# Row sums and turned attention outputs by way of device memory, in a fused graph-attention kernel

## The chip, the cores and the metric

One of the eight cores of a Trainium2 chip runs the whole program. The metric is the device time of one execution in microseconds (us). A core has five engines with instruction streams of their own: TensorE (PE, with PEld for its weight loads), VectorE (DVE), ScalarE (ACT), GpSimd (POOL) and SyncE (SP), whose queue issues nearly all transfers here. All times below are in us where no unit is named.

## The reference

Two layers on x of shape (32, 512, 512), with one 512 x 512 adjacency matrix for all 32 sequences. The first is masked attention with eight heads of 64, the second a graph convolution; each is followed by a residual and a layer norm.

```python
q, k, v = x @ Wq + bq, x @ Wk + bk, x @ Wv + bv          # eight heads of 64
scores = einsum('bihd,bjhd->bhij', q, k) / sqrt(64) + where(adj == 0, -1e9, 0)
weights = softmax(scores, axis=-1)
x = layernorm(x + einsum('bhij,bjhd->bihd', weights, v))
y = einsum('nm,bmd->bnd', adj, x)
x = layernorm(x + einsum('bnd,do->bno', y, W1) + b1)
```

## The kernel before

The kernel works through the 32 sequences b. The eight heads are taken in pairs hp (two heads of 64 lanes fill 128 partitions) and two pairs make a group g, so there are 64 groups (b, g), numbered i in the main loop. Every engine's order is the order in which the Python code emits instructions; there is no scheduler behind it. In one pass of the loop over groups:

- `attend(b, hp)`: 16 matmuls (32 instructions, L585 for the two pairs) multiply the exponentials e with the values into one PSUM bank, which holds the output transposed (head lanes on partitions, queries along the row). There are eight banks, used in a ring.
- `fold_squares(b, hp)`: the sum over the keys of the exponentials es (already added over the four key blocks on GpSimd, L576) still lies across partitions. VectorE transposes es in 32 x 32 squares (L618) and adds up each run of 32 (L620), which leaves, for every query, four parts on four different partitions, 32 apart.
- `turn_out(b, hp)`: VectorE transposes the output in 32 x 32 squares into `attT` (L601); 16 transfers on SP (L606), each of one square column of 16 KB, carry the squares to their partitions in `rows`. That is 32 transfers in a group.
- `scores` for the next group: 32 matmul instructions (L561) into 16 banks, which VectorE masks and evacuates (L563) and ACT exponentiates (L565).
- `add_up(b, g)`: four small matmuls (eight instructions, L628) with a constant 0/1 matrix `fold` (four identity matrices of 32 stacked) add the four parts into a PSUM bank. VectorE takes the reciprocal (L631) and adds the sums into `sums` (L632); GpSimd adds the reciprocals into `inverses` (L633). `sums` and `inverses` are looked at once, at the end (`judge`, L662 to L669), to decide whether a slower general kernel has to run.
- then the slot of the group, a list of units: projections of sequence b + 1 (L353), convolutions and aggregations of sequence b - 1 (L353, L472), statistics (L415), splits into high and low parts (L441, L445), `scale_rows` (ACT multiplies `rows` by the inverses, L644) and `add_rows` (GpSimd adds them to x, L648).

Two places differ from this. In the first group the second fold comes after the scores, and `add_up` is put at place 8 of the slot. In the last sequence both folds of its second group lie in the slots, and after the last slot come `add_up(31, 1)`, `last_residual` (L654 to L657, multiplying by the inverse), the statistics of the first norm, and the last aggregation and convolution. `load_squares` (L248) reads the x of two sequences ahead in 32-wide columns, `store` and `load` (L456, L233) write a finished sequence and read x for the residual; all three are on SP.

Of the kernel before, what the change touches and what calls it, by code (L numbers as in the profile page):

```python
# [37 lines left out]
FP = mybir.dt.float32  # L38
# [4 lines left out]
ALU = mybir.AluOpType  # L43
AX = mybir.AxisListType
# [3 lines left out]
P = 128  # L48
# [10 lines left out]
SQ = 32  # L59
XIN = 4  # L60
GROUP = 4
# [146 lines left out]
def fast_kernel(ctx: ExitStack, tc, verdict, x, adj, Wq, bq, Wk, bk, Wv, bv, W1, b1, out):  # L208
    nc = tc.nc
    B, N, D = x.shape  # L210
    H = Wq.shape[1] // HD
    HP = H // 2
    NB = N // P
# [4 lines left out]
    consts = ctx.enter_context(tc.tile_pool(name="consts", bufs=1))  # L218
    work = ctx.enter_context(tc.tile_pool(name="work", bufs=2))
    psum = ctx.enter_context(tc.tile_pool(name="psum", bufs=1, space=bass.MemoryType.PSUM))  # L220
    ctx.enter_context(tc.manual_schedule())

    def bank(*shape):

        return psum.tile([P, *shape], FP, name="bank", tag="bank", bufs=8)
# [34 lines left out]
    ident = consts.tile([P, P], FP, name="ident")  # L260
    make_identity(nc, ident)
    ones = consts.tile([P, 1], FP, name="ones")
    nc.gpsimd.memset(ones, 1.0)

    fold = consts.tile([P, SQ], FP, name="fold")
    nc.gpsimd.tensor_add(fold, ident[:, 0:SQ], ident[:, SQ:2 * SQ])
    for i in (2, 3):
        nc.gpsimd.tensor_add(fold, fold, ident[:, i * SQ:(i + 1) * SQ])
    eps = consts.tile([P, 1], FP, name="eps")
    nc.gpsimd.memset(eps, EPS)  # L270
    zero = consts.tile([P, 1], FP, name="zero")
# [2 lines left out]
    sums = consts.tile([P, NB, GROUP], FP, name="sums")  # L274
# [115 lines left out]
    def flips(b):  # L390

        return [(turn_squares if b else x_transpose, b, c) for c in range(NB)] + [(sum_rows, b)] if b < B else []

    def projections(b):


        if b >= B:
            return []
        units = [(project, b, which, i) for which in "qkv" for i in ORDER]
        for n in (5, 12):  # L400
            units[n:n + 4] = units[n + 2:n + 4] + units[n:n + 2]
        return units
# [136 lines left out]
    def aggregation(b):  # L539


        return [[(f, b, d) for d in range(DB)] if b >= 0 else [] for f in (split, aggregate)]

    def convolution(b):
        return [(convolve, b, i) for i in (1, 2, 5, 6, 7, 3, 4)] if b >= 0 else []


    E, ES, OUT, AT, ROWS, SQUARES, PART, INVERSE = {}, {}, {}, {}, {}, {}, {}, {}
    PAIRS = GROUP // 2

    def scores(b, g):
# [41 lines left out]
    def turn_out(b, hp):  # L593

        po = OUT.pop((b, hp))
        at = AT[b, hp] = work.tile([P, N], FP, name="attT")
        if (b, hp // PAIRS) == (B - 1, HP // PAIRS - 1):
            nc.scalar.activation(at, po, AF.Copy)
            return

        nc.vector.transpose(at, po)  # L601
        turned = at.rearrange("p (c j f) -> p c j f", c=NB, j=P // SQ)
        rows = ROWS[b, hp] = work.tile([P, NB, P], FP, name="rows")
        for i in range(P // SQ):
            for j in range(P // SQ):
                nc.sync.dma_start(rows[j * SQ:(j + 1) * SQ, :, i * SQ:(i + 1) * SQ],  # L606
                                  turned[i * SQ:(i + 1) * SQ, :, j, :])

    def fold_squares(b, hp):

        if hp % PAIRS == 0:
            PART[b, hp // PAIRS] = work.tile([P, GROUP, N // SQ], FP, name="part", bufs=1)
        if (b, hp // PAIRS) == (B - 1, HP // PAIRS - 1):

            square = work.tile([P, 2, N], FP, name="v", bufs=3)
        else:
            square = SQUARES.pop((b, hp))
        nc.vector.transpose(square.rearrange("p s n -> p (s n)"), ES.pop((b, hp)).rearrange("p s n -> p (s n)"))  # L618
        heads = slice(2 * (hp % PAIRS), 2 * (hp % PAIRS) + 2)
        nc.vector.tensor_reduce(PART[b, hp // PAIRS][:, heads, :], square.rearrange("p s (j f) -> p s j f", f=SQ),  # L620
                                axis=AX.X, op=ALU.add)

    def add_up(b, g):

        part = PART.pop((b, g)).rearrange("p h (j i) -> p i j h", i=P // SQ)
        pm = bank(NB, GROUP)
        for i in range(P // SQ):
            nc.tensor.matmul(pm[i * SQ:(i + 1) * SQ, :, :], fold, part[:, i, :, :], start=True, stop=True,  # L628
                             tile_position=(0, i * SQ))
        inverse = INVERSE[b, g] = work.tile([P, NB, GROUP], FP, name="inverse")  # L630
        nc.vector.reciprocal(inverse, pm)  # L631
        nc.vector.tensor_add(sums, pm, sums)  # L632
        nc.gpsimd.tensor_add(inverses, inverses, inverse)  # L633

    def inverse_of(b, hp):
# [37 lines left out]
    def run(units):  # L673
        for unit in units:
            unit[0](*unit[1:])
# [4 lines left out]
    pm = bank(P)  # L680
    for _ in range(7):
        nc.tensor.matmul(pm, still, still, start=True, stop=True)
    turned, first = flips(0), projections(0)
# [38 lines left out]
    def norm(t, which):  # L722

        if t - which < 0:
            return []
        lo, hi = which * NB, (which + 1) * NB
        return [(square_root, t, slice(lo, hi)), (invert_root, t, slice(lo, hi))] + [
            (normalise, t, slot) for slot in range(lo, hi)]

    def folds(b, g):  # L730
        return [(fold_squares, b, hp) for hp in range(g * PAIRS, (g + 1) * PAIRS)]
# [9 lines left out]
    def merge(units, behind):  # L741

        merged = []
        for k in range(max(len(units), len(behind))):
            merged += units[k:k + 1] + (behind[k] if k < len(behind) else [])
        return merged

    def units_of(b):

        made, turned = projections(b + 1), flips(b + 2)  # L750
        splits, gathered = aggregation(b - 1)
        old, seen = norm(b - 1, 1), survey(b - 2)

        fresh, young = ([(statistics, b - 1, 0, c) for c in range(NB)], norm(b - 1, 0)) if b else ([], [])
        scaled, added = residuals(b, 0)
        if b == B - 1:


            first, second = folds(b, 1)
            behind = [fresh[:2], fresh[2:], young[:1] + scaled[:1], young[1:3], young[3:5] + [first],  # L760
                      young[5:] + splits[:1], splits[1:] + scaled[1:]]
            return [merge(convolution(b - 2), behind), [second] + added + gathered]

        ready = [(turn_over, b)] if b > 1 else []
        if old:
            behind = [seen[:2], seen[2:], old[:2], old[2:4] + fresh[:2], old[4:] + ready + fresh[2:]] + [
                [u] for u in young]
        elif b:
            behind = [ready + fresh] + [[u] for u in young]
            behind += [[(look_for_low_half, c)] for c in range(NB)]  # L770
        else:
            behind = [[]] + [[(sum_weights, w1, n)] for n in range(4)]
        behind += [[] for _ in range(11 - len(behind))]
        behind += [splits[:1], scaled + added, splits[1:2]]
        slot0 = merge(made[:16], behind)
        values = made[16:]
        scaled, added = residuals(b, 1)
        slot1 = values[:3] + gathered[:1] + splits[2:3] + gathered[1:2] + splits[3:] + scaled[:1]
        slot1 += values[3:]
        if b == B - 2 > 0:  # L780
            slot1 += [(load, B - 1)]
        slot1 += gathered[2:3] + turned[:1] + gathered[3:]
        convolved = convolution(b - 1) if b < B - 2 else []
        slot1 += merge(convolved, [scaled[1:] + added[:1] + turned[1:2], turned[2:3], turned[3:4], [], [], [],
                                   added[1:] + turned[4:]])
        return [slot0, slot1]

    GROUPS = H // GROUP
    groups = [(b, g) for b in range(B) for g in range(GROUPS)]
    for i, (b, g) in enumerate(groups):  # L790
        for hp in range(g * PAIRS, (g + 1) * PAIRS):
            attend(b, hp)
            if i < len(groups) - 1 and (i or hp == 0):
                fold_squares(b, hp)
            turn_out(b, hp)
            if i == hp == 0:
                run(flips(1))
        if g == 0:
            slots = units_of(b)
        if i < len(groups) - 1:  # L800
            later = scores(*groups[i + 1])
            if i:
                add_up(b, g)
            else:
                fold_squares(b, 1)
                slots[0].insert(8, (add_up, b, g))
        if g == 0 and b + 2 < B:
            load_squares(b + 2)
        for unit in slots[g]:
            run([unit])  # L810
            if unit[0] == convolve or unit[0] == project and unit[3] == 7:
                run(later)
                later = []
        run(later)
        later = []
# [41 lines left out]
    for unit in last:  # L857
# [13 lines left out]
        if unit[2] == 7:  # L871
            pm = bank(N)
# [41 lines left out]
```

## Time and profile before

| | us |
|---|---|
| median of three runs | 2749.52 (2749.11 to 2749.98) |
| the profiled execution's own time | 2749.17 |
| its span in the trace | 2747.3 |
| TensorE busy | 2729.7 (99%), granted clock 0.998 |
| VectorE, GpSimd, ScalarE busy | 2064.8, 1903.0, 1411.4 |
| transfers: share of the 16 DMA engines | 23.0%, mean 52 GB/s |

The span is what the trace covers; the execution's own time has 1.9 more around it. A busy time of TensorE is not a measure of full use, because matmuls overlap and their ends are modelled: the start of the next one says more. In a timeline a line reads: start, length of the group of instructions, engine, line of the program, operation, output<-inputs, shapes, number, and in brackets how long the engine stood idle before it and what ended that. In the list of transfers, the row transfers are 2016 of 16 KB with 1.8 from issue to landing, the column loads of x 496 of 64 KB with 2.4, and the four stores of 256 KB at the end 2.7.

### The profile page before, as it was taken

The numbers are of one execution on the slowest core, as the hardware profiler recorded it, in microseconds if no ns is written. First come the engines' busy times: TensorE is split into PE (matmuls) and PEld (weight loads), VectorE is DVE, ScalarE is ACT, GpSimd is POOL, SyncE is SP. The second block draws the span as 40 slices with busy tenths as digits, with TensorE's granted clock in tenths as the row PEclk, the third lists the DMA queues.
The fourth block names the chain that finished last, engine by engine and source line by source line (L and its number), as shares of the span: only waits on it lengthen the run. The fifth ranks groups of instructions, "written<-read, shape, count | busy, mean of one in ns | idle before, by whom it ended". The sixth has DMA issues, their size and how long they took to land.

```text
span 2747.3 us, 39383 instructions
## 1 busy us (share of the span) xinstructions
PE 2729.7 (99%) x12856; PEld 1911.3 (70%) x12856; DVE 2064.8 (75%) x3348; ACT 1411.4 (51%) x2459; POOL 1903.0 (69%) x1224
## 2 busy tenths in 40 slices
PE   9999999999999999999999999999999999999997
PEld 6676676766767767667676676676766767767666
DVE  6777777777777787777877777777777777777777
ACT  3455464554544655446555455454554644555454
POOL 4776677666867667777677676777666867667775
PEclk9999999999999999999999999999999999999999
DMA  5212211222212222122221222211222212222121
GB/s 149 32 28 62 56 29 45 57 62 57 44 30 56 61 59 54 19 57 60 60 57 23 51 59 61 56 27 47 58 62 57 43 30 56 62 58 49 25 59 50
DMA packets 592915, 142.20 MB, mean 52 GB/s; under 512 B 554560, under 2 KB 558656, under 8 KB 592704
## 3 DMA queue, kind: packets, MB, share of 16 engines
q1 hardware_dynamic: 592704, 139.63, 23.0%
q8 instruction: 103, 1.69, 0.3%
q14 instruction: 108, 0.88, 0.1%
HBM read 72.88 MB, written 33.55 MB: 39 GB/s over the span
## 4 chain that ended last, share of the span: by engine, by line
PE 98%; DVE 1%; DMA 0%; ACT 0%; issue 0%; SPq 0%; POOL 0%; DVEq 0%; ACTq 0%
PE bank L353 56%; PE bank L561 17%; PE bank L585 16%; PE bank L472 8%; PE bank L628 0%; DMA wq<-in_L_gnn_Wq_dram 0%; DVE bnst L415 0%; DVE xs L534 0%; DVE part L847 0%; PE bank L287 0%; POOL xs L532 0%; SPq L239 0%; ACT xT L430 0%; DVE stat L416 0%; DVE xT L534 0%
## 5 line engine op out<-in xcount | busy, mean ns | idle before, releaser
L565 ACT ACTIVATE e<-e 128x1024 f32<-128x1024 f32 x512 | 524.9, 1053 | 572.8 <-DVE e L563 537.5
L563 DVE SCALAR_TENSOR_TENSOR e<-gap,bank 128x512 f32<-128x512 uint8 x1024 | 617.7, 679 | 20.2 <-PE bank L561 20.2
L576 POOL TENSOR_TENSOR es<-es,e 128x1024 f32<-128x1024 f32 x256 | 618.3, 2415 | 20.1
L576 POOL TENSOR_TENSOR es<-e 128x1024 f32<-128x1024 f32 x128 | 316.2, 2470 | 328.2 <-ACT e L565 328.2
L561 PE MATMUL bank<-q,k 64*128 64x512 f32 x2048 | 463.0, 598 | 0.0
L585 PE MATMUL bank<-e,v 128*64 128x512 f32 x2048 | 453.6, 595 | 0.0
L353 PE MATMUL bank<-wv,xT 128*128 128x256 f32 x1792 | 405.4, 381 | 0.0
L353 PE MATMUL bank<-xT,wk 128*128 128x256 f32 x1792 | 402.9, 379 | 0.0
L353 PE MATMUL bank<-xT,wq 128*128 128x256 f32 x1792 | 400.8, 381 | 1.9 <-DMA wq<-in_L_gnn_Wq_dram 1.7
L353 PE MATMUL bank<-w,yT 128*128 128x256 f32 x1792 | 394.3, 380 | 3.5 <-DVE yT L509 3.5
L561 PEld LDWEIGHTS bank<-q,k 64*128 64x128 f32 x2048 | 203.4, 186 | 258.0 <-issue 152.2
L353 PEld LDWEIGHTS bank<-w,yT 128*128 128x128 f32 x1792 | 341.2, 191 | 52.0 <-DVE yT L509 3.9
L353 PEld LDWEIGHTS bank<-xT,wk 128*128 128x128 f32 x1792 | 340.2, 190 | 46.1
L353 PEld LDWEIGHTS bank<-xT,wq 128*128 128x128 f32 x1792 | 337.8, 190 | 48.9 <-issue 1.9
L353 PEld LDWEIGHTS bank<-wv,xT 128*128 128x128 f32 x1792 | 337.6, 190 | 47.6 <-DVE e L563 0.8
L644 ACT ACTIVATE rows<-rows,zero,inverse 128x64 f32<-128x64 f32 x1008 | 343.4, 427 | 4.6 <-DMA rows<-attT 4.6
L585 PEld LDWEIGHTS bank<-e,v 128*64 128x64 f32 x2048 | 141.4, 137 | 277.1 <-issue 275.7
L648 POOL TENSOR_TENSOR xs<-xs,rows 128x512 f32<-128x512 f32 x124 | 158.0, 1285 | 164.3 <-DMA xs<-in_x_dram 164.3
L565 ACT ACT_TABLE_LOAD x30 | 38.5, 1283 | 416.6 <-DVE e L563 416.6
L445 DVE TENSOR_TENSOR low<-xs,high 128x512 fp32r<-128x512 f32 x122 | 141.8, 1162 | 106.1 <-ACT high L441 106.1
L534 DVE TENSOR_TENSOR xs<-bank,xs 128x512 f32<-128x512 f32 x186 | 124.3, 682 | 96.8 <-PE bank L353 46.2
L430 ACT ACTIVATE xs<-xs,shift,rstd 128x512 f32<-128x512 f32 x248 | 181.9, 803 | 27.2 <-DVE shift L425 27.2
(128 smaller groups left out, 2963.3 us busy)
## 6 DMA issues: line engine op xcount, KB each, us to landing
rows<-attT SPq DMA_DIRECT2D x2016, 16.0 KB, 1.8
xin<-in_x_dram SPq DMA_DIRECT2D x496, 64.0 KB, 2.4
xs<-in_x_dram SPq DMA_DIRECT2D x31, 1024.0 KB, 5.1
out_dram<-xs SPq DMA_DIRECT2D x31, 1024.0 KB, 4.4
xin<-in_x_dram SPq DMA_DIRECT2D x4, 256.0 KB, 3.3
wq<-in_L_gnn_Wq_dram SPq DMA_DIRECT2D x2, 512.0 KB, 6.7
wk<-in_L_gnn_Wk_dram SPq DMA_DIRECT2D x2, 512.0 KB, 5.7
yT<-in_adj_dram SPq DMA_DIRECT2D x1, 1024.0 KB, 7.2
```

Source lines behind the costliest of these rows:

```text
L353: nc.tensor.matmul(pm[:, r, :], left[:, d, r * P:(r + 1) * P], right[:, d, :], start=(d == 0), stop=(d == 1))
L430: nc.scalar.activation(row, row, AF.Identity, bias=SHIFT[t][:, slot:slot + 1], scale=RSTD[t][:, slot:slot + 1])
L445: nc.vector.tensor_sub(LOW[b, d], cols, HIGH[b, d].bitcast(FP))
L472: nc.tensor.matmul(pm.rearrange("p a n -> p (a n)"), part, adjT[:, n % NB, :], start=(n == 0), stop=(n == 2 * NB - 1))
L534: nc.vector.tensor_add(block, pm, block)
L561: nc.tensor.matmul(ps[s], keys[:, j * P:(j + 1) * P], queries, start=True, stop=True)
L563: nc.vector.scalar_tensor_tensor(e[:, s, :], gap[:, j, :], NEG * root, ps[s], op0=ALU.mult, op1=ALU.add)
L565: nc.scalar.activation(e, e, AF.Exp, scale=1.0 / root)
L576: nc.gpsimd.tensor_add(ES[b, hp], ES[b, hp] if j > 1 else E[b, hp, 0], E[b, hp, j])
L585: nc.tensor.matmul(po[s * HD:(s + 1) * HD, :], values, e[:, s, :], start=(j == 0), stop=(j == NB - 1))
L644: nc.scalar.activation(part, part, AF.Identity, bias=zero, scale=inverse[:, c, s:s + 1])
L648: nc.gpsimd.tensor_add(cols, cols, ROWS.pop((b, hp)))
```

## The change

A pool `passing` of tiles in device memory is added. The turned output `attT` is stored there whole (one transfer), and a new `fetch_rows` reads it back in four transfers, one for each 32 partitions, each of 512 pieces of 128 bytes. The four parts of the row sums take the same way: a store after the second fold, and a new `fetch_parts` with four reads, after which each partition holds all four parts of its queries. `add_up` is then a reduction on VectorE; the matrix `fold` and its matmuls are gone, and so is their PSUM bank. `sums` is added from the reduced tile in SBUF instead of from PSUM. For the new layout of the parts each reduction of 1024 elements becomes two of 512. In the main loop the fetches are emitted around the second `turn_out`, and `add_up` moves from directly behind the scores to place 3 of the slot (place 8 stays in the first group). In the last group the fetch follows the last fold, and `add_up` keeps its place.

```diff
-    fold = consts.tile([P, SQ], FP, name="fold")
-    nc.gpsimd.tensor_add(fold, ident[:, 0:SQ], ident[:, SQ:2 * SQ])
-    for i in (2, 3):
-        nc.gpsimd.tensor_add(fold, fold, ident[:, i * SQ:(i + 1) * SQ])
...
         nc.vector.transpose(at, po)
-        turned = at.rearrange("p (c j f) -> p c j f", c=NB, j=P // SQ)
+        TURNED[b, hp] = passing.tile([P, N], FP, name="turned")
+        nc.sync.dma_start(TURNED[b, hp], at)
+
+    def fetch_rows(b, hp):
         rows = ROWS[b, hp] = work.tile([P, NB, P], FP, name="rows")
-        for i in range(P // SQ):
-            for j in range(P // SQ):
-                nc.sync.dma_start(rows[j * SQ:(j + 1) * SQ, :, i * SQ:(i + 1) * SQ],
-                                  turned[i * SQ:(i + 1) * SQ, :, j, :])
+        turned = TURNED.pop((b, hp)).rearrange("(i r) (c j f) -> j r c i f", r=SQ, c=NB, f=SQ)
+        for j in range(P // SQ):
+            nc.sync.dma_start(rows[j * SQ:(j + 1) * SQ, :, :].rearrange("p c (i f) -> p c i f", f=SQ), turned[j])
...
-        heads = slice(2 * (hp % PAIRS), 2 * (hp % PAIRS) + 2)
-        nc.vector.tensor_reduce(PART[b, hp // PAIRS][:, heads, :], square.rearrange("p s (j f) -> p s j f", f=SQ),
-                                axis=AX.X, op=ALU.add)
+        for s in range(2):
+            nc.vector.tensor_reduce(part[:, :, :, 2 * (hp % PAIRS) + s].rearrange("p i c -> p c i"),
+                                    square[:, s, :].rearrange("p (c i f) -> p c i f", c=NB, f=SQ), axis=AX.X,
+                                    op=ALU.add)
+        if hp % PAIRS == PAIRS - 1:
+            PASSED[b, hp // PAIRS] = passing.tile([P, P // SQ, NB * GROUP], FP, name="passed")
+            nc.sync.dma_start(PASSED[b, hp // PAIRS], part.rearrange("p i c h -> p i (c h)"))
+
+    def fetch_parts(b, g):
+
+        part = PART[b, g].rearrange("p a c h -> p a (c h)")
+        passed = PASSED.pop((b, g)).rearrange("(a r) i x -> i r a x", r=SQ)
+        for i in range(P // SQ):
+            nc.sync.dma_start(part[i * SQ:(i + 1) * SQ, :, :], passed[i])

     def add_up(b, g):

-        part = PART.pop((b, g)).rearrange("p h (j i) -> p i j h", i=P // SQ)
-        pm = bank(NB, GROUP)
-        for i in range(P // SQ):
-            nc.tensor.matmul(pm[i * SQ:(i + 1) * SQ, :, :], fold, part[:, i, :, :], start=True, stop=True,
-                             tile_position=(0, i * SQ))
         inverse = INVERSE[b, g] = work.tile([P, NB, GROUP], FP, name="inverse")
-        nc.vector.reciprocal(inverse, pm)
-        nc.vector.tensor_add(sums, pm, sums)
+        nc.vector.tensor_reduce(inverse, PART.pop((b, g)).rearrange("p a c h -> p c h a"), axis=AX.X, op=ALU.add)
+        nc.vector.tensor_add(sums, sums, inverse)
+        nc.vector.reciprocal(inverse, inverse)
         nc.gpsimd.tensor_add(inverses, inverses, inverse)
...
             first, second = folds(b, 1)
+            fetched = [(fetch_parts, b, 1)]
...
-            return [merge(convolution(b - 2), behind), [second] + added + gathered]
+            return [merge(convolution(b - 2), behind), [second] + fetched + added + gathered]
...
                 fold_squares(b, hp)
+            if hp % PAIRS == PAIRS - 1 and i < len(groups) - 1:
+                fetch_rows(b, hp - 1)
+                if i:
+                    fetch_parts(b, g)
             turn_out(b, hp)
             if i == hp == 0:
                 run(flips(1))
+            if hp % PAIRS == PAIRS - 1 and i < len(groups) - 1:
+                fetch_rows(b, hp)
...
             later = scores(*groups[i + 1])
-            if i:
-                add_up(b, g)
-            else:
+            if i == 0:
                 fold_squares(b, 1)
-                slots[0].insert(8, (add_up, b, g))
+                fetch_parts(b, g)
+            slots[g].insert(3 if i else 8, (add_up, b, g))
```

More of the change, by code (lines that the diff above doesn't have):

```diff
@@ L220, in fast_kernel @@
     psum = ctx.enter_context(tc.tile_pool(name="psum", bufs=1, space=bass.MemoryType.PSUM))
+    passing = ctx.enter_context(tc.tile_pool(name="passing", bufs=2, space=bass.MemoryType.DRAM))
     ctx.enter_context(tc.manual_schedule())
@@ L545, in convolution @@
         return [(convolve, b, i) for i in (1, 2, 5, 6, 7, 3, 4)] if b >= 0 else []
-    E, ES, OUT, AT, ROWS, SQUARES, PART, INVERSE = {}, {}, {}, {}, {}, {}, {}, {}
+    E, ES, OUT, AT, ROWS, SQUARES, PART, INVERSE, TURNED, PASSED = ({} for _ in range(10))
     PAIRS = GROUP // 2
@@ L601, in turn_out @@
         nc.vector.transpose(at, po)
-        turned = at.rearrange("p (c j f) -> p c j f", c=NB, j=P // SQ)
+        TURNED[b, hp] = passing.tile([P, N], FP, name="turned")
+        nc.sync.dma_start(TURNED[b, hp], at)
+    def fetch_rows(b, hp):
         rows = ROWS[b, hp] = work.tile([P, NB, P], FP, name="rows")
-        for i in range(P // SQ):
-            for j in range(P // SQ):
-                nc.sync.dma_start(rows[j * SQ:(j + 1) * SQ, :, i * SQ:(i + 1) * SQ],
-                                  turned[i * SQ:(i + 1) * SQ, :, j, :])
+        turned = TURNED.pop((b, hp)).rearrange("(i r) (c j f) -> j r c i f", r=SQ, c=NB, f=SQ)
+        for j in range(P // SQ):
+            nc.sync.dma_start(rows[j * SQ:(j + 1) * SQ, :, :].rearrange("p c (i f) -> p c i f", f=SQ), turned[j])
     def fold_squares(b, hp):
         if hp % PAIRS == 0:
-            PART[b, hp // PAIRS] = work.tile([P, GROUP, N // SQ], FP, name="part", bufs=1)
+            PART[b, hp // PAIRS] = work.tile([P, P // SQ, NB, GROUP], FP, name="part", bufs=1)
+        part = PART[b, hp // PAIRS]
         if (b, hp // PAIRS) == (B - 1, HP // PAIRS - 1):
```

## The prediction

> **What bounds the kernel now.** I read the page's busy times and chain first, then the timeline of TensorE around one fold, of VectorE around the same place, and of the end. The page:
>
> ```profile
> PE 2729.7 (99%) x12856; PEld 1911.3 (70%) x12856; DVE 2064.8 (75%) x3348; ACT 1411.4 (51%) x2459; POOL 1903.0 (69%) x1224
> ...
> PE 98%; DVE 1%; DMA 0%; ACT 0%; issue 0%; SPq 0%; POOL 0%; DVEq 0%; ACTq 0%
> ```
>
> TensorE carries the chain: a microsecond taken from its instructions is a microsecond of the span, while one saved elsewhere is worth nothing until it reaches TensorE. The one TensorE item that the change touches is the fold (L628), here between the scores and the next projection, in the timeline of TensorE; the last two lines are a place where no fold stands between:
>
> ```profile
> 1020.31 7.21 PE L561 MATMUL bank<-q,k 64*128 64x512 f32 x32
> 1027.44 0.26 PE L628 MATMUL bank<-part,fold 128*32 128x16 f32 x8
> 1027.64 5.45 PE L353 MATMUL bank<-wv,xT 128*128 128x256 f32 x24
> ...
> 38.97 7.21 PE L561 MATMUL bank<-q,k 64*128 64x512 f32 x32
> 46.11 8.90 PE L353 MATMUL bank<-wv,xT 128*128 128x256 f32 x40
> ```
>
> Starts, not durations, give the price: the fold holds TensorE from 1027.44 to 1027.64 (0.190 in nearly all 64), and the scores before it take 7.13 to 7.14 with a fold next (1020.31 to 1027.44) and 7.14 without one (38.97 to 46.11). So the fold costs its own 0.19 and nothing around it.
>
> VectorE at the same place, with its waits:
>
> ```profile
> 1018.87 1.22 DVE L620 TENSOR_REDUCE part<-e 128x32 f32<-128x1024 f32 x1
> 1020.42 0.72 DVE L601 STREAM_TRANSPOSE attT<-bank 128x512 f32<-128x512 f32 x1 [0.34 <-PE bank L585]
> 1021.47 9.65 DVE L563 SCALAR_TENSOR_TENSOR e<-gap,bank 128x512 f32<-128x512 uint8 x16 [0.33 <-PE bank L561]
> 1031.04 0.25 DVE L631 RECIPROCAL inverse<-bank 128x16 f32<-128x16 f32 x1
> 1031.21 0.11 DVE L632 TENSOR_TENSOR sums<-bank,sums 128x16 f32<-128x16 f32 x1
> ```
>
> VectorE waits for TensorE 0.34 and then 0.33: that is all the room the two row-sum folds have in a group, and it is the same in nearly every group. The end is different (VectorE, then GpSimd at two places):
>
> ```profile
> 2695.51 1.22 DVE L620 TENSOR_REDUCE part<-v 128x32 f32<-128x1024 f32 x1
> ...
> 2699.53 0.11 DVE L632 TENSOR_TENSOR sums<-bank,sums 128x16 f32<-128x16 f32 x1
> 2699.72 0.70 DVE L655 TENSOR_TENSOR bank<-bank,inverse 128x512 f32<-128x512 f32 x1
> ...
> 2720.02 1.18 DVE L668 TENSOR_TENSOR well<-well 128x1 f32<-128x1 f32 x1
> ...
> 2678.65 4.80 POOL L576 TENSOR_TENSOR es<-es,e 128x1024 f32<-128x1024 f32 x2
> ```
>
> In the chain of waits the stretch 2699.03 to 2723.07 is VectorE (with a few ACT and POOL steps), no longer TensorE: residual, statistics, normalise, split, verdict, then the last convolution. What delays L655 there delays the end one for one.
>
> [...] from the last scores matmul start to the next start it is 0.52 instead of 0.22, with fold or without[...]. [...] a reduction of 512 elements takes 0.686 and one of 1024 takes 1.220, so halving costs 2 x 0.686 - 1.220 = 0.15. [...] L632, with one input in PSUM, takes 0.11 always; L668, a single element per partition but both in SBUF, took 1.18 beside GpSimd's additions. [...] The SP queue shows such waits before: 115.5 us in 29 loads behind their stores.
>
> **The change part by part.**
> *Fold matmuls gone.* 62 folds between scores and projection or convolution: 62 x 0.190 = 11.8. The fold of (0,0) lies inside a projection run and also costs a switch on each side: that run of 40 plus the fold takes 9.02 up to 78.19, 40 matmuls unbroken 8.64: 0.38. The fold of (31,1) falls in the end, where TensorE isn't the limit: nothing. Together **-12.2**. The building of the matrix goes from POOL at 2 us, off the chain.
>
> *Reductions halved* (two of 512 for one of 1024): back to back they start 0.61 apart, against 1.14 for the long one when backlogged, so 0.07; unpipelined 0.15. Per group 0.14 to 0.30, inside the first wait of 0.34, and 0.33 more follows: nothing. In the two groups of sequence 1 (at 127 and 170) VectorE has no wait there and TensorE already stalls: all of it shows, 2 x 0.14 to 0.30, say **+0.4**.
>
> *add_up on VectorE, three units later.* Before: 0.25 + 0.11. After: a reduction of 64 elements (nearest: L662, 16 elements, 0.14; I take 0.15 to 0.2), the addition to sums, now both in SBUF (0.1 free, up to a whole GpSimd instruction, 1.3 or 2.4), and a reciprocal (0.18 to 0.25). In g = 1 it lands near 1033.8, where VectorE then waits 2.3 for ACT; in g = 0 near 1075.4, when GpSimd has finished L576 at 1075.1. Behind it are evacuations of banks of which TensorE has eight: over 8 us of cover. Zero, except at (31,0), below.
>
> *SP queue and transfers.* 32 issues of 0.60 per group (19 us) become 2 stores, 8 row fetches, a store of the parts and 4 part fetches: 15 x about 0.55 = 8 us (a 512-piece issue like the xin loads takes 0.53), plus two waits of about 2 us. Queued behind those waits are the other rows, the xin loads, store and load of xs: all still earlier than before. Only VectorE waits for the parts: in the group at 1056 the second reduction ends at 1062.8, the store goes out by 1063.1, four row issues take SP to 1065.5, four part issues to 1067.9, and with 1.8 to land that is 1069.7, wanted at 1075.4. At (0,0) VectorE will wait until about 81, but it has 3.8 idle up to 83.75. Rows landing earlier cover nothing: ACT waited 4.6 for them in the whole run, off the chain.
>
> *The end.* (31,0): the addition to sums comes at about 2678.9 and meets L576 (2678.4 to 2680.9: 0.2 earlier than shown, as L633 no longer goes ahead of it, and 2.4 for each of the two): 2.0 of stall, in a stretch with little idle time up to the last fold; about 1.9 arrives there, with 0.2 for the halved reductions. Then the last fold no longer feeds TensorE: its parts go out (0.1 to start; a store lands in 2.0 at best in the trace), SP wakes (0.1), four fetches of which the last is issued 3 x 0.6 later and lands in 1.8 (as the 128-piece row transfers do), VectorE wakes (0.1): 5.9, then add_up 0.45. Before, L655 started 2.99 after that fold's end (2696.73). Sum: 1.9 + 0.2 + 5.9 + 0.45 - 2.99 = **+5.5**. Bounds: 2 (no stall, quick landings) to 8 (store 2.7, fetches 2.4, late starts).
>
> Sum: -12.2 + 0.4 + 5.5 = -6.3 on the profiled execution's 2749.2 gives 2742.9; the median of the runs stands 0.35 above it: **2743**.
>
> **Rivals.**
> *The end is hidden* (0.15): if other work fills the trip, only -12 + 1 is left: 2738. Against: the chain already runs on VectorE there.
> *VectorE becomes the limit in every group, slower* (0.08): if the halved reductions with their regrouped output cost over 0.33 each beyond the long one, the 0.67 of room is spent and TensorE's last scores, which wait for evacuations, slip. At 0.53 each (two full 0.686, waits of 0.15 each, against the pipelined 1.14) that is (1.06 - 0.67) x 62 = +24, so 2767. It decides for slower from 0.38 each. Against: the measured difference is 0.07 to 0.15.
> *The switch keeps what the fold used* (0.05): TensorE saves nothing, only the end is paid: 2755. Against: 7.14 both ways.
>
> **How the numbers follow.** A difference of 0.2% (5.5 us) is about what a measurement of this kernel can tell. My main case (0.72) runs from 2739.5 to 2745.5, three quarters of it below 2744. Faster: 0.54 + 0.15, less a little for what I don't see, 0.66; same 0.24; slower 0.10. Range 2737 to 2748: the hidden end below, and above it a longer trip at the end with small losses per group.
>
> **What would show it.** Right: no TensorE work between L561 and the next line, 7.14 from scores to projection; VectorE's wait before the second attT down from 0.34 to 0.04 to 0.20 and before the scores still 0.33; a stall of about 2 in the addition to sums near (31,0); VectorE idle for some 5 before the last add_up, and TensorE idle before the last aggregation. Wrong: the 0.33 gone and scores longer than 7.2 in ordinary groups, or waits of VectorE for the parts in mid-run.

## The result and the profile after

The changed kernel takes 2744.18 us (median of 19 runs, 2743.0 to 2746.4) against 2750.35 for the kernel before: a ratio of 0.9979 (95% interval 0.9973 to 0.9985), 6 us faster. The profiled execution took 2743.55 with a span of 2741.7, 5.6 less than before; 0.6 of that is there at the first scores already. It belongs to the loading at the start, not to the change: over the traces of all runs here the first scores begin anywhere from 37.98 to 41.95.

TensorE's timeline in a middle group, where a fold stood between the scores and the projection:

```profile
1009.02 7.09 PE L582 MATMUL bank<-e,v 128*64 128x512 f32 x32
1016.04 7.21 PE L558 MATMUL bank<-q,k 64*128 64x512 f32 x32
1023.18 5.02 PE L350 MATMUL bank<-wv,xT 128*128 128x256 f32 x22
```

From the start of the scores to the projection it is 7.14, as it was to the fold: the fold's time is gone and nothing took its place. VectorE in the same group, first around the halved reductions (now L621, two to a fold), then at the new `add_up`:

```profile
1014.60 1.28 DVE L621 TENSOR_REDUCE part<-e 128x16 f32<-128x512 f32 x2
1016.16 0.72 DVE L599 STREAM_TRANSPOSE attT<-bank 128x512 f32<-128x512 f32 x1 [0.28 <-PE bank L582]
1017.20 9.65 DVE L560 SCALAR_TENSOR_TENSOR e<-gap,bank 128x512 f32<-128x512 uint8 x16 [0.32 <-PE bank L558]
...
1029.27 0.26 DVE L638 TENSOR_REDUCE inverse<-part 128x16 f32<-128x64 f32 x1
1029.56 0.94 DVE L639 TENSOR_TENSOR sums<-sums,inverse 128x16 f32<-128x16 f32 x1
1030.53 0.25 DVE L640 RECIPROCAL inverse<-inverse 128x16 f32<-128x16 f32 x1
1031.68 0.71 DVE L442 TENSOR_TENSOR low<-xs,high 128x512 fp32r<-128x512 f32 x1 [0.89 <-ACT high L438]
```

A pair of reductions is 0.06 longer than the one before, so the first wait for TensorE shrank from 0.34 to 0.28 and the second stayed. The addition to `sums`, 0.11 before, takes 0.94 here; VectorE still waits 0.89 for ACT behind it. The end of the run:

```profile
2667.62 1.78 DVE L639 TENSOR_TENSOR sums<-sums,inverse 128x16 f32<-128x16 f32 x1
...
2686.17 1.28 DVE L621 TENSOR_REDUCE part<-v 128x16 f32<-128x512 f32 x2
...
2688.25 0.42 DVE L474 TENSOR_TENSOR yT<-bank,yT 128x256 f32<-128x256 f32 x1 [0.47 <-ACT yT L472]
2692.18 0.26 DVE L638 TENSOR_REDUCE inverse<-part 128x16 f32<-128x64 f32 x1 [3.50 <-DMA part<-passed]
2692.47 1.09 DVE L639 TENSOR_TENSOR sums<-sums,inverse 128x16 f32<-128x16 f32 x1
2693.59 0.25 DVE L640 RECIPROCAL inverse<-inverse 128x16 f32<-128x16 f32 x1
2693.95 0.70 DVE L663 TENSOR_TENSOR bank<-bank,inverse 128x512 f32<-128x512 f32 x1
```

From the end of the last fold (2687.45) to the multiplication by the inverse (2693.95; L655 before) it is 6.50; it was 2.99.

Because the work repeats exactly, the two traces can be laid over each other at the starts of the 64 scores. Counted from the first scores, the changed kernel is 0.39 ahead after the first group, then gains 0.185 a group, 0.19 in a clean one; in sequence 1 two groups fall short of that by 0.07 and 0.78; at the last scores it is 10.8 ahead, and one more fold (0.19) follows. From there to the end of the span it loses 6.0. So 11.9 gained, 0.9 lost in sequence 1, 6.0 lost at the end, and 0.6 from the start: 5.6.

### The profile page after: what moved, and what is told of

The parts are those of the page before. It is cut to its first block, busy times and chain, and to the rows that moved or that the text cites. A ratio compares the mean times of both kernels' runs of the same rounds, so it can differ in the third digit from the quotient of the medians.

```text
span 2741.7 us, 36328 instructions
## 1 busy us (share of the span) xinstructions
PE 2720.6 (99%) x12344; PEld 1903.7 (69%) x12344; DVE 2145.6 (78%) x3540; ACT 1411.0 (51%) x2459; POOL 1914.2 (70%) x1221
## 4 chain that ended last, share of the span: by engine, by line
PE 96%; DVE 2%; DMA 0%; ACT 0%; POOL 0%; issue 0%; SPq 0%; DVEq 0%; ACTq 0%
PE bank L350 56%; PE bank L558 17%; PE bank L582 16%; PE bank L469 8%; DVE bnst L412 0%; DVE e L560 0%; DMA wq<-in_L_gnn_Wq_dram 0%; DVE xs L531 0%; DVE xT L531 0%; DVE k L442 0%; POOL xs L529 0%; ACT xs L427 0%; DVE sums L639 0%; DVE stat L413 0%; DVE part L861 0%
## 5 line engine op out<-in xcount | busy, mean ns | idle before, releaser
L573 POOL TENSOR_TENSOR es<-e 128x1024 f32<-128x1024 f32 x128 | 316.5, 2473 | 481.1 <-ACT e L562 481.1
L573 POOL TENSOR_TENSOR es<-es,e 128x1024 f32<-128x1024 f32 x256 | 618.9, 2418 | 20.1
L442 DVE TENSOR_TENSOR low<-xs,high 128x512 fp32r<-128x512 f32 x122 | 163.1, 1337 | 61.5 <-ACT high L438 61.5
L443 POOL TENSOR_TENSOR xs<-xs,b_r 128x512 f32<-128x512 f32 x124 | 157.4, 1282 | 21.5 <-DVE low L442 21.5
```

The source lines that it names most:

```text
L442: nc.vector.tensor_sub(LOW[b, d], cols, HIGH[b, d].bitcast(FP))
L443: nc.gpsimd.tensor_add(cols, cols, b1_r[:, None, d * P:(d + 1) * P].to_broadcast([P, NB, P]))
L573: nc.gpsimd.tensor_add(ES[b, hp], ES[b, hp] if j > 1 else E[b, hp, 0], E[b, hp, j])
```

## The experiments

The theory (A in the expectations): the gain is the fold's time on TensorE, and half of it is given back at the end, where VectorE waits for the parts' trip. Rivals: the gain comes from the transfers (B), the end is limited anyway and the loss lies in the groups (C). In the diffs below, `...` stands for what is left out.

**The rows alone through device memory.** The kernel before with `fetch_rows`; folds, reductions and `add_up` as before.

```diff
-        for i in range(P // SQ):
-            for j in range(P // SQ):
-                nc.sync.dma_start(rows[j * SQ:(j + 1) * SQ, :, i * SQ:(i + 1) * SQ], ...)
+        TURNED[b, hp] = passing.tile([P, N], FP, name="turned")
+        nc.sync.dma_start(TURNED[b, hp], at)
...
```

> The kernel before with the attention outputs alone passing through device memory; the row sums stay with TensorE's fold and add_up stays behind the scores. Theory A (the gain is the 63 fold matmuls taken off TensorE, 0.19 each; 5.9 of it is given back at the end): nothing is gained, 0 within 1 us of before, the fold's 0.19 is still there in every group. Theory B (the gain comes from 32 transfers becoming 10 on the SP queue and rows that arrive earlier): about 6 us faster than before.

Measured: 2748.91 against 2750.1, ratio 0.9997 (0.9989 to 1.0005). In the trace its 64 scores stay within 0.04 of the kernel before, counted from the first. The rows' new way gains nothing by itself; B falls. (Behind the last scores this trace is 1.5 longer than the one before; the last section comes back to that.)

**The parts alone through device memory.** The changed kernel with the 32 row transfers of before.

```diff
-        for j in range(P // SQ):
-            nc.sync.dma_start(rows[...].rearrange("p c (i f) -> p c i f", f=SQ), turned[j])
+        for i in range(P // SQ):
+            for j in range(P // SQ):
+                nc.sync.dma_start(rows[j * SQ:(j + 1) * SQ, :, i * SQ:(i + 1) * SQ], ...)
...
```

> The changed kernel with the attention outputs going from SBUF to SBUF in 32 transfers a group as before; only the parts of the row sums pass through device memory. Theory A: as the changed kernel, 6 us (5 to 7) faster than before, though the store of the parts now stands behind 16 row transfers, so that VectorE may wait some 1 us for the parts in g = 0, hidden behind the banks. Theory B: the gain is gone, 0 within 1 us of before.

Measured: 2829.15, ratio 1.0283 (1.0269 to 1.0297): 79 us slower, which neither theory had. SP's timeline in this kernel shows the store of the parts behind 16 row transfers:

```profile
1049.19 10.87 SPq L604 DMA_DIRECT2D rows<-attT  x16
1060.17 0.53 SPq L624 DMA_DIRECT2D passed<-part  x1
1061.86 1.75 SPq L631 DMA_DIRECT2D part<-passed  x4
```

The reduction had ended at 1048. (The row transfers themselves began 3.6 late, since SP waited for GpSimd's L654, which reads an older `rows`.) VectorE comes to `add_up` at 1061.5 in g = 1 and stands; the splits behind it come late (its timeline), and TensorE, which needs their low parts for the aggregation, waits too (TensorE's timeline):

```profile
1064.95 0.26 DVE L636 TENSOR_REDUCE inverse<-part 128x16 f32<-128x64 f32 x1 [3.48 <-DMA part<-passed]
1065.24 1.06 DVE L637 TENSOR_TENSOR sums<-sums,inverse 128x16 f32<-128x16 f32 x1
...
1066.51 5.54 DVE L442 TENSOR_TENSOR low<-xs,high 128x512 fp32r<-128x512 f32 x2
```
```profile
1069.30 1.20 PE L469 MATMUL bank<-adjT,low 128*128 128x512 f32 x4 [1.36 <-DVE low L442]
...
1072.10 1.19 PE L469 MATMUL bank<-adjT,low 128*128 128x512 f32 x4 [0.67 <-DVE low L442]
```

In all, VectorE waits 135.7 for the parts and TensorE 65 for the low parts. In the changed kernel the same store follows the reduction at once, in SP's timeline:

```profile
1015.91 0.34 SPq L626 DMA_DIRECT2D passed<-part  x1
1016.36 2.60 SPq L607 DMA_DIRECT2D rows<-turned  x4
1019.00 2.06 SPq L633 DMA_DIRECT2D part<-passed  x4
```

**The same with `add_up` later**, to test that reading.

```diff
-            slots[g].insert(3 if i else 8, (add_up, b, g))
+            slots[g].insert(8 if i == 0 else 7 if g and b else 3, (add_up, b, g))
```

> The run with the parts alone through device memory (28 in a thousand slower than before), with one edit: in g = 1 add_up stands at place 7 of the slot, behind the two splits and directly ahead of scale_rows, instead of place 3. Theory D (in that run VectorE waits 3.5 for the parts in g = 1, since their store stands behind 16 row transfers; the splits behind it come late and TensorE waits for their low parts): by place 7 the parts have landed, TensorE no longer waits for the low parts, and most of the 79 us goes: 2745 to 2755. Rival E (the rows that come late, or the transfers as such, cost the time): it stays above 2800.

Measured: 2752.35, ratio 1.0009 (1.0000 to 1.0017). 77 of the 79 us went with a place in the order of VectorE's work: the wait behind `add_up` was the cause, not the transfers as such. What this kernel still lacks of the changed one is in the trace 1.2 in sequence 1, some 4 spread over the groups and 3.3 at the end (1.4 of that are slow steps of TensorE, as in the last section).

**The last group without the trip.** The fold matrix and its matmuls return for (31,1) alone; its store and its fetch go.

```diff
...
+        if (b, g) == (B - 1, GROUPS - 1):
...
+            for i in range(P // SQ):
+                nc.tensor.matmul(pm[i * SQ:(i + 1) * SQ, :, :], fold, part[:, i, :, :], start=True, stop=True,
+                                 tile_position=(0, i * SQ))
+            nc.vector.reciprocal(inverse, pm)
...
```

> The changed kernel, with the parts of the last group (31,1) alone added up by TensorE with the fold matrix as before, so without the trip through device memory at the end. Theory A: VectorE's wait of 3.5 for the parts and the blocked addition of 1.1 go; the multiplication in last_residual follows the last reduction of the folds after about 3.0 instead of 6.5; 3.5 us faster than the changed kernel, 9.5 faster than before. Theory C (the end is limited by TensorE or other work in any case, and the missing gain was lost in the groups): within 1 us of the changed kernel.

Measured: 2738.75, ratio 0.9956 (0.9942 to 0.9969); 5.4 faster than the changed kernel where 3.5 was expected. VectorE at its end:

```profile
2686.05 1.28 DVE L625 TENSOR_REDUCE part<-v 128x16 f32<-128x512 f32 x2
2687.25 0.42 DVE L478 TENSOR_TENSOR yT<-bank,yT 128x256 f32<-128x256 f32 x1
2688.12 0.42 DVE L478 TENSOR_TENSOR yT<-bank,yT 128x256 f32<-128x256 f32 x1 [0.45 <-ACT yT L476]
...
2688.81 0.70 DVE L677 TENSOR_TENSOR bank<-bank,inverse 128x512 f32<-128x512 f32 x1
```

From the last reduction's end (2687.33) to the multiplication it is now 1.48, not 3.0: the kernel before waits for ACT in that place (0.44 and 1.44), and a VectorE that arrives 2.4 late waits less. The delay from (31,0) is mostly swallowed there when there is no trip, and counts in full when there is one. Against 6.50 with the trip that is 5.0 of the 6.0 lost at the end. C falls.

**The addition to `sums` on GpSimd.**

```diff
-        nc.vector.tensor_reduce(inverse, PART.pop((b, g)).rearrange("p a c h -> p c h a"), axis=AX.X, op=ALU.add)
-        nc.vector.tensor_add(sums, sums, inverse)
-        nc.vector.reciprocal(inverse, inverse)
+        total = work.tile([P, NB, GROUP], FP, name="total")
+        nc.vector.tensor_reduce(total, PART.pop((b, g)).rearrange("p a c h -> p c h a"), axis=AX.X, op=ALU.add)
+        nc.vector.reciprocal(inverse, total)
+        nc.gpsimd.tensor_add(sums, sums, total)
```

> The changed kernel with the addition to sums moved from VectorE to GpSimd (the reduction goes into a tile of its own, total). Theory A: the stall of 1.8 in VectorE at (31,0) and of 1.1 in the last add_up go, and both lie on the path that sets the end: 2 to 3 us faster than the changed kernel, 8 to 9 faster than before; in all other groups nothing changes. Theory C: within 1 us of the changed kernel.

Measured: 2742.51, ratio 0.9969 (0.9957 to 0.9981). The medians say 1.7 faster than the changed kernel, the ratios to before 2.7, and their intervals overlap. In the trace, from VectorE's first scores evacuation of the last group to the multiplication by the inverse, it is 37.3 against 40.2, so 2.9 less, as expected. But only 1.8 of it is left at the end of the span. The last convolution on TensorE, in the changed kernel and then in this one, and VectorE's next wait behind it, in the same order:

```profile
2717.30 8.47 PE L350 MATMUL bank<-w,yT 128*128 128x256 f32 x38 [2.72 <-DVE yT L506]
2717.59 10.78 PE L350 MATMUL bank<-w,yT 128*128 128x256 f32 x38 [5.29 <-DVE yT L506]
...
2719.59 0.69 DVE L531 TENSOR_TENSOR xT<-bank,xT 128x512 f32<-128x512 f32 x1 [1.09 <-ACT mix L521]
2721.25 0.69 DVE L531 TENSOR_TENSOR xT<-bank,xT 128x512 f32<-128x512 f32 x1 [2.46 <-ACT mix L521]
```

TensorE had waited longer here, nine of its next steps took 0.43 instead of 0.22, and VectorE stood 1.4 longer for them (last section).

**The fold left out altogether**, from the kernel before: the four parts are not added up at all.

```diff
-        for i in range(P // SQ):
-            nc.tensor.matmul(pm[i * SQ:(i + 1) * SQ, :, :], fold, part[:, i, :, :], ...)
-        nc.vector.reciprocal(inverse, pm)
-        nc.vector.tensor_add(sums, pm, sums)
+        nc.vector.reciprocal(inverse, part[:, 0, :, :])
+        nc.gpsimd.tensor_add(sums, sums, part[:, 0, :, :])
```

> The kernel before without the fold matmuls and with nothing in their place: add_up takes the reciprocal of one of the four parts, and the addition to sums is on GpSimd. It leaves out the adding up of the four parts across partitions. Theory A: what the fold costs TensorE, with no trip at the end: 12 us (11 to 13) faster than before, 0.19 per group in the trace. Theory B or C (the fold is hidden, or the gain lies elsewhere): less than 4 us.

Measured: 2739.62, ratio 0.9965 (0.9952 to 0.9979), 10 faster, a little short of the 11 to 13 expected. In the trace it is 10.9 ahead at the last scores, counted from the first, where the changed kernel is 10.8: what the changed kernel gains in the groups is what leaving the fold out gains, some 0.18 a group. The last 1 us is lost in its end, in the place just shown: TensorE has waited 3.82 there, goes 0.43 a step, and VectorE waits 2.46 where it waited 1.25 before.

**VectorE's room in a group**, two sizes. A reduction is repeated in sequences 2 to 30: 256 elements in the second fold, or 512 in both. The larger:

```diff
+        if 1 < b < B - 1:
+            nc.vector.tensor_reduce(part[:, :, :, 2 * (hp % PAIRS)].rearrange("p i c -> p c i"),
+                                    square[:, 0, :].rearrange("p (c i f) -> p c i f", c=NB, f=SQ), axis=AX.X,
+                                    op=ALU.add)
```

> The changed kernel with one more reduction of 256 elements on VectorE (a repeat) in the second fold of each group of sequences 2 to 30. Theory A: VectorE's two waits for TensorE in a group, 0.28 and 0.33 in the changed kernel, leave 0.61 of room; the repeat takes about 0.35 to 0.42 per group: within 1 us of the changed kernel, the wait before the second attT gone. Rival (VectorE already sets the pace of the scores): 58 x 0.4 = 23 us slower than the changed kernel.

Measured: 2745.22, ratio 0.9982 (0.9976 to 0.9989): no difference from the changed kernel that these runs can tell. The repeat takes 0.36 of VectorE's time, and the wait before the second attT (0.28) is gone.

> The changed kernel with one of the two reductions of 512 elements repeated in each of the two folds of a group of sequences 2 to 30: 2 x 0.61 to 0.69 = 1.2 to 1.4 per group. Theory A: 0.6 to 0.8 more than the room of 0.61, and all of that falls on TensorE's scores: 58 x 0.6 to 0.8 = 35 to 46 us slower than the changed kernel, the waits before the second attT and before the scores gone. If TensorE had more cover than the two waits show: no change.

Measured: 2760.2, ratio 1.0038 (1.0024 to 1.0051): 16 slower than the changed kernel, less than half of what was expected. VectorE's and TensorE's timelines in this kernel:

```profile
1020.32 1.28 DVE L621 TENSOR_REDUCE part<-e 128x16 f32<-128x512 f32 x2
1021.51 0.68 DVE L625 TENSOR_REDUCE part<-e 128x16 f32<-128x512 f32 x1
1022.11 0.71 DVE L599 STREAM_TRANSPOSE attT<-bank 128x512 f32<-128x512 f32 x1
1022.74 4.83 DVE L560 SCALAR_TENSOR_TENSOR e<-gap,bank 128x512 f32<-128x512 uint8 x8
...
1021.28 7.47 PE L558 MATMUL bank<-q,k 64*128 64x512 f32 x32
1028.68 5.45 PE L350 MATMUL bank<-wv,xT 128*128 128x256 f32 x24
```

No wait is left, and the scores take 7.40 to 7.41 instead of 7.14: 58 x 0.27 = 15.7, and at the last scores the trace is 15.4 behind the changed kernel's, as measured. The repeats add 2 x 0.6 = 1.19, but the first evacuation starts only 0.30 later after TensorE's first scores (1.46 against 1.16). So the room was 0.89, not the 0.61 of the two waits: where nothing is waited for, an instruction starts some 0.08 before its forerunner's recorded end (1021.51 to 1022.11 is 0.60 for a reduction of 0.68). That counts at three places, before both attT and before the scores.

**All three mends together**: the last group on TensorE, `sums` on GpSimd, and one reduction of 1024 elements for the two (the output written as `part[:, :, :, heads].rearrange("p i c s -> p s c i")`).

> The changed kernel with three edits: the last group added up by TensorE (the fold matrix built in a free xin buffer in the last sequence), the addition to sums on GpSimd, and one reduction of 1024 elements instead of two of 512 in each fold. Theory A: the end costs under 1 us against before, and the stalls of sequence 1 shrink by 0.3 to 0.6: 1 us (0 to 2) faster than the run with the last group alone on TensorE, 12 faster than before.

Measured: 2738.46 (2736.6 to 2740.3), ratio 0.9960 (0.9947 to 0.9974): 12 faster than before and 6 faster than the changed kernel, whose 19 runs do not reach down to it. Against the run with the last group alone on TensorE it is 0.3 in the medians, which these runs can't tell from nothing. In the trace the end now costs nothing (0.5 gained from the last scores on, the fold aside).

## Why the prediction was right, point by point

The forecast of 2743 and the range held, and the mechanism is the one it named: the fold's time gained in the groups, and about half of it paid at the end for a trip on VectorE's chain. That the sums agree so closely is in part luck, as the last but one point shows. Step by step:

- *Fold matmuls gone, 62 x 0.19 + 0.38 = 12.2.* Measured 0.39 for (0,0) and 0.185 a group, 11.9. The reading of starts rather than durations was right: 7.14 on both sides.
- *Halved reductions, hidden in the groups.* Right: 0.06 for a pair, below even the lower bound of 0.07. In sequence 1, forecast 0.4, it is 0.85. The second of its two groups loses 0.78, and two pairs of reductions are only 0.12 of that. Its splits came to lie beside GpSimd's additions: L442 took 1.79 and 1.56 there, L445 0.68 and 1.44 before. The run with `sums` on GpSimd loses 0.45 in sequence 1, with splits of 0.68 and 1.45: so the other 0.4 came with the addition to `sums`, which the forecast took to be hidden everywhere but in the end.
- *`add_up` hidden behind the banks.* Hidden (VectorE waits for the parts at (0,0), 1.0, and at the end, and nowhere else), but with less to spare than I said. I saw VectorE's 2.3 of waiting for ACT in g = 1 and added "over 8 us of cover" by the eight banks behind it. That is wrong for g = 1: the next that TensorE needs there is the low part of a split, and the 2.3 are all the cover there is. The changed kernel fits into it; the kernel with the parts alone did not, and lost 79 us.
- *SP queue: rows that arrive earlier cover nothing.* True of the rows themselves, and incomplete: the few row transfers are what lets the parts reach VectorE in time. I priced the queue for the changed kernel and not for its absence.
- *The end, +5.5.* Measured 6.0, with three terms off that nearly cancel: +0.3, -1.2 and +1.3. The delay that arrives from (31,0) is 2.4 (forecast 2.1; the stall itself 1.8, forecast 2.0). The trip is 4.7 (forecast 5.9): the store landed after 1.5, not 2.0, and the fetches left 0.44 apart, not 0.6. The last `add_up` took 1.8 (forecast 0.45), mostly because GpSimd, with L315 from 2689.81, was in the way of L639 after all: 1.09 instead of 0.1. That the trip was priced too high and the addition too low is luck.
- *Rivals.* That the switch from the scores to the next line keeps what the fold used, and that the end is hidden, are both excluded by the traces: from the start of the last scores matmul to the next start it is 0.52 after all 64 scores of either kernel, and the end loses 6.0. That VectorE becomes the limit did not happen; its point was set too low: not 0.67 of room but 0.89 beyond what the changed kernel uses.

The forecast of the stall at (31,0) had little behind it in the trace of before: L668, with both inputs in SBUF, took 1.18 there and ended 0.02 after one of GpSimd's additions (L495), while L632, with one input in PSUM, took 0.11 or 0.12 in all 64 groups with GpSimd busy beside each of them. That the addition to `sums` would wait for L576 in the same way was the author's estimate. The runs agree with it: the addition of 16 elements took 1.78 beside L573, 1.09 beside L315, and nothing from VectorE once it was on GpSimd, which brought the multiplication at the end forward by 2.9.

## What to carry to other kernels

When a chain moves a small step off the limiting engine and over a transfer, the middle of the run may hide the trip while the end does not, as here (11.9 gained, 6.0 lost at the end): keep the short way for the last round. Before calling a wait hidden, find what stands behind the waiting instruction on its own engine and which of those results the limiting engine needs first; and where GpSimd is busy, keep one operand of a small VectorE addition in PSUM (0.11 or 0.12 here, against up to 1.78 with both in SBUF), or give it to GpSimd.

## What the runs showed of the hardware

A store of 32 KB to device memory landed after 1.5 us and a read of 8 KB from it after 1.8 (medians of the changed kernel's 64 and 256), no slower than the 16 KB transfers within SBUF of the kernel before (1.8): the trip there and back with four reads took 4.7 us at the end.

The addition to `sums` (L639, 16 elements in a partition, both inputs in SBUF) took 0.17 or 0.18 in 30 of the 64 groups of the changed kernel. In the other 34 GpSimd was in the middle of an instruction when the addition began; the addition then ended 0.03 to 0.04 after that instruction and took 0.27 to 1.78. Before, with one input in PSUM, it took 0.11 or 0.12 in all 64.

TensorE's granted clock fell to half beside an idle stretch at the end. Three stretches of the changed kernel:

```profile
2690.00:2703.00 13.00, 10.55 (x49) 8.93 (x47) 8.81 (x20) 2.42 (x5) 3.75 (x4) 0.99 0.02 2
2703.00:2710.00 7.00, 6.21 (x15) 4.97 (x16) 5.83 (x10) 3.93 (x6) 3.08 (x2) 0.53 0.01 2
2710.00:2720.00 10.00, 7.28 (x33) 5.77 (x32) 8.73 (x21) 1.98 (x4) 7.84 (x8) 1.00 0.00 1
```

The columns after the length are the busy times of PE, PEld, DVE, ACT and POOL with the number of instructions, then the granted clock (0.99, 0.53, 1.00), the share of the DMA engines and GB/s. TensorE had waited 3.24 for the low parts up to 2703.79, and twelve steps of its aggregation then went 0.43 apart, where the run with the last group on TensorE, with no such wait in that place, went 0.23. It cost nothing here, since VectorE's chain was later still. Nor is it the change's doing; the kernel before has seven such steps in its last convolution, from the seventh on:

```profile
2723.07 10.16 PE L353 MATMUL bank<-w,yT 128*128 128x256 f32 x38 [3.49 <-DVE yT L509]
```

In seven of the eleven traces the slow steps came at once in the last convolution, and VectorE's wait there was 2.46, against 1.09 to 1.43 in the other four. The runs with the rows alone, with the fold left out and with `sums` on GpSimd are among the seven; the kernel before, the changed kernel, the run with the last group on TensorE and the one with all three mends are the four. So single traces can differ by 1.0 to 1.4 us in their end for this alone. The length of the wait is not all that decides it: after 3.24 the slow steps came at once in the changed kernel's aggregation, after 3.48 in the last convolution of the run with all three mends none came. What else does, these runs do not show.
